# Three loads of the gate begun inside the next image's first norm, and two elementwise steps of the side work on GpSimd

## The chip, the cores and the metric

The kernel runs on one core of one Trainium2 chip. The metric is the time of one execution on the device in microseconds (us); where several executions are given, the median is used. A core has five engines that run side by side and wait for one another through semaphores: TensorE (PE; its weight loads are listed as PEld), VectorE (DVE), ScalarE (ACT), GpSimd (POOL) and SyncE (SP). In this kernel SP only issues DMA transfers. Each engine works through its own queue in order, so an instruction that waits holds up all that stand behind it on the same engine.

## What is computed

The input is 16 images of 256 channels by 32 x 32 positions, that is 256 x 1024 numbers an image, all in f32. Two layers follow one another, each behind a group norm:

```
x = x + attention_layer(group_norm(x))        # position, layer norm, 4 heads, feed-forward
x = x + scan_layer(group_norm(x))
# the scan layer, for one image:
xs    = xs + rel_h + rel_w
ctx   = sigmoid(conv3(xs) + gate_b)            # 256 channels
u, z  = split(xs @ in_proj.T)                  # 512 channels each
u     = silu(causal_conv4(u) + conv_b)
dt, Bm, Cm = split(u @ x_proj.T)
delta = softplus(dt @ dt_proj.T + dt_b)
h[t]  = exp(delta[t] * A) * h[t-1] + delta[t] * u[t] * Bm[t]    # 512 channels x 64 states
ys[t] = sum over states of h[t] * Cm[t]
y     = (ys + u * D) * silu(z)
out   = (y @ out_proj.T) * ctx
```

The two lines of code that change engine belong to `tok = group_norm(x) + position` at the head of the attention layer and to the product with `silu(z)` at the tail of the scan layer.

## The kernel before, in words

**The scan sets the beat.** The recurrence of one image has 512 x 64 rows of 1024 steps. They are cut into 256 units of 128 rows. The units of all images run one after another, 4096 in all, in the loop that begins at line 1000. Each unit takes one round of the loop, and a round writes, in this order:

- `load(n+6)` (line 900): SP fetches the unit's two rows of `delta*u`, spread over 128 partitions, into a buffer `dub`. There are seven such buffers; the one that is taken is free once `scan(n-1)` has read it.
- `inputs(n+4)` (line 905): POOL multiplies `dub` in place by `bt`, the rows of Bm.
- a step of `outputs` for the block of eight units that ended last (lines 947 to 963, on PE and ACT), which ends with two small stores to `ys` (line 970).
- `scan(n)` (line 922): DVE runs the recurrence over `a` (in PSUM) and `dub`.
- `decay(n+2)` (lines 914 and 916): PE spreads the pieces of delta into PSUM, and ACT takes the exponential. There are two buffers `a`, so the decay of unit n+2 can only begin when scan n is done.
- side work, below.

**The side work** is all that is not recurrence. While image b is scanned, the side work is, in this order: `first_norm(b+1)`, `gate_and_store(b-1)`, `attention_layer(b+1)`, `scan_inputs(b+1)`. Each is a generator that writes a few instructions and then yields a share; a share below 1 is that many rounds, and a larger one is at least one round and is divided by a rate (`gap`, `rate_for`, lines 980 to 988), which is chosen so that all shares of an image fill 247 rounds. The list GATE (line 811) gives the shares of `gate_and_store` for that sum. Image 0's side work runs alone ahead of the loop; while image 0 is scanned there is no gate; while image 15 is scanned there is only the gate of image 14; the gate of image 15 runs after the loop.

**The order on each engine.** PE, ACT, DVE and POOL keep the order in which the program writes their instructions (lines 1054 to 1058). On SP the compiler may put a transfer earlier, as long as its buffer and its data allow.

**The steps that the change touches.** `first_norm` sums both halves of the image (line 261), subtracts the mean (line 280), squares on ACT, sums again, takes the root on ACT (lines 291, 292) and multiplies (line 295); `along` writes one transfer after each step as long as there are some (two loads of the position). Then two DVE additions (line 362) make `tok`, and two stores keep it in DRAM (line 363). `gate_and_store` fetches `ys`, `w_o`, `ud` and `zs` of the first of four row groups, with a share of 0.4 after each (lines 822 to 824); then for each row group d it writes a load, the DVE instruction of line 830 (`us = us*D + ys`), a load, the DVE product of line 834 (`us = us*zs`), a load. The loads are three items further in the list each time. PE then multiplies by `w_o` (line 859) in eight steps, and DVE applies the gate and the residual (lines 846, 848). In the profile all tiles of the `wide` pool that a `fetch` fills are called `xs`; `xs<-ud` is the load of u for line 830, and `xs<-zs` that of z for line 834. The pool has ten buffers.

Of the kernel before, what the change touches and what calls it, by code (L numbers as in the profile page):

```python
# [14 lines left out]
ALU = mybir.AluOpType  # L15
# [14 lines left out]
ND = DI // P  # L30
# [20 lines left out]
def attention_then_scan_kernel(  # L51
# [18 lines left out]
    nc = tc.nc  # L70
    B = x.shape[0]
# [36 lines left out]
    def psum(name, dims=P):  # L108
        return (bank(mm, name) if beside["scan"] else free_bank(name))[:dims]
# [4 lines left out]
    def psum3(name):  # L114
        return bank(next(three), name) if beside["scan"] else free_bank(name)

    def work(name, n=L):
        return wide.tile([P, L + 2 + CONV], F32, name=name, tag="wide")[:, :n]
# [4 lines left out]
    def hs(h):  # L123
        return ts(h, HL)
# [6 lines left out]
    def col(name, i=0, n=1):  # L131
        o, w = _COLS[name]
        assert i + n <= w
        return vec[:, o + i : o + i + n]
# [104 lines left out]

    def along(steps, fetches):  # L240
        for share in steps:
            if fetches:
                fetches.pop(0)()
            yield share
        assert not fetches

    def grouped(ap):
        return ap.rearrange("p (h g t) -> p h g t", g=NG, t=2)

    def over_group(s):  # L250
        return s.unsqueeze(1).unsqueeze(3).to_broadcast([P, L // (2 * NG), NG, 2])
# [6 lines left out]
    def group_norm(src, dst):  # L258
        def sum_of(part, s, k):
            view = part.rearrange("p (h g t) -> p g h t", g=NG, t=2)  # L260
            nc.vector.tensor_reduce(s[:, k, :], view, AX.XY, ALU.add)

        def mean_of(s, name):
            m = psum(f"{name}_ps")[:, :NG]
            for k in range(KC):
                nc.tensor.matmul(m, avg, s[:, k, :], start=(k == 0), stop=(k == KC - 1))
            return m

        per = C / (C * L / NG)
        s = small.tile([P, KC, NG], F32, name="gn_s", tag="gn_s")  # L270
        sum_of(src[0], s, 0)
        yield 1
        sum_of(src[1], s, 1)
        m = mean_of(s, "gn_m")
        yield 1
        s = small.tile([P, KC, NG], F32, name="gn_q", tag="gn_s")
        qs = []
        nc.vector.tensor_scalar(m, m, per, None, ALU.mult)
        for k in range(KC):
            nc.vector.tensor_tensor(grouped(dst[k]), grouped(src[k]), over_group(m), ALU.subtract)  # L280
            q = work("gn_sq")
            nc.scalar.activation(q, dst[k], AF.Square)
            qs.append(q)
            yield 1
        sum_of(qs[0], s, 0)
        yield 1
        sum_of(qs[1], s, 1)
        del qs, q
        v = mean_of(s, "gn_v")
        yield 1  # L290
        nc.scalar.activation(v, v, AF.Ln, bias=eps, scale=per)
        nc.scalar.activation(v, v, AF.Exp, scale=-0.5)
        yield 2.2
        for k in range(KC):
            nc.vector.tensor_tensor(grouped(dst[k]), grouped(dst[k]), over_group(v), ALU.mult)
            yield 0.6
# [42 lines left out]
    state = [dict() for _ in range(B)]  # L339
# [6 lines left out]
    def fetches(to, src, n=KC):  # L346
        return [partial(fetch, to, src, k) for k in range(n)]


    def first_norm(b):  # L350
        xs, tok = [], []
        kept = state[b]["kept"] = dram.tile([C, L], F32, name="kept", tag="kept")
        if "x" in state[b]:
            xs = state[b].pop("x")
        else:
            for go in fetches(xs, x[b]):
                go()
            yield 0.4
        gn = [work("gn") for _ in range(KC)]
        yield from along(group_norm(xs, gn), fetches(tok, pos))  # L360
        for k in range(KC):
            nc.vector.tensor_tensor(tok[k], tok[k], gn[k], ALU.add)
            nc.sync.dma_start(kept[ts(k, P), :], tok[k])
            yield 0.6

# [442 lines left out]
        st["ys"] = dram.tile([DI, L], F32, name="ys", tag="ys")  # L808
        yield 1

    GATE = [0.4] * 4 + ([0.6, 0.6, 0.4] * ND)[:-1] + [1.3] * 8 + [1]

    def gate_and_store(b):
        st = state[b]
        (wo_s,), bring = weights((w_o, ND))
        ys, us, zs, gs, xs = [], [], [], [], []
        come = [
            partial(fetch, to, st[name], d)
            for d in range(ND) for to, name in ((ys, "ys"), (us, "ud"), (zs, "zs"))
        ]  # L820
        come.insert(1, bring[0])
        for go in come[:4]:
            go()
            yield 0.4
        come = come[4:] + [
            partial(fetch, to, st[name], k) for k in range(KC) for to, name in ((gs, "gs"), (xs, "xr"))
        ]
        for d in range(ND):
            come.pop(0)()
            nc.vector.scalar_tensor_tensor(us[d], us[d], col("D", d), ys[d], ALU.mult, ALU.add)  # L830
            ys[d] = None
            yield 0.6
            come.pop(0)()
            nc.vector.tensor_tensor(us[d], us[d], zs[d], ALU.mult)  # L834
            zs[d] = None
            yield 0.6
            if d + 1 < ND:
                come.pop(0)()
                yield 0.4
        if b + 2 < B:  # L840
            come += fetches(state[b + 2].setdefault("tok", []), state[b + 2]["kept"])
        ready = []

        def finish():
            for o, hf, ps in ready:
                nc.vector.scalar_tensor_tensor(ps, gs[o][:, hs(hf)], 1.0, ps, ALU.add, ALU.mult)
                t = xs[o][:, hs(hf)]
                nc.vector.scalar_tensor_tensor(t, ps, 0.25, t, ALU.mult, ALU.add)
                if hf == 1:
                    nc.sync.dma_start(out[b, ts(o, P), :], xs[o])  # L850
            ready.clear()

        for o in range(KC):
            for hf in range(2):
                ps = psum3("m_ps")
                for q in range(2):
                    first = o * HL + hf * 2 + q
                    for d in range(ND):
                        nc.tensor.matmul(  # L859
                            ps[:, ts(q, C)], us[d][:, ds(first, P, 4)], wo_s[:, d, :],  # L860
                            start=(d == 0), stop=(d == ND - 1),
                        )
                    if q == 1:
                        finish()
                    if come:
                        come.pop(0)()
                    yield 1.3
                ready.append((o, hf, ps))
        finish()
        del ps  # L870
        yield 1
        st.clear()


    units = [
# [27 lines left out]
    def inputs(n):  # L903
        v = loaded[n]
        nc.gpsimd.tensor_tensor(v, v, blocks[units[n][0]]["bt"], ALU.mult)  # L905
# [66 lines left out]
    def prepare(b):  # L972
        return chain(first_norm(b), attention_layer(b), scan_inputs(b))
# [6 lines left out]
    def gap(share, rate):  # L980
        return share if share < 1 else max(1.0, share / rate)
# [18 lines left out]
    for n, (b, k, q, e, i) in enumerate(units):  # L1000
        at = n % UNITS
        if at == 0:
            parts = [prepare(b + 1)] if b + 1 < B else []
            total = steps * len(parts)
            if b > 0:
                parts = [first_norm(b + 1), gate_and_store(b - 1), attention_layer(b + 1), scan_inputs(b + 1)]
                if b + 1 == B:
                    parts = parts[1:2]
                total = total + GATE
            side = chain(*parts)  # L1010
            rate, due = rate_for(total, UNITS - AHEAD - 3), 0.0
        if at == UNITS - AHEAD:
            for _ in side:
                pass
            if b + 2 < B:
                for go in fetches(state[b + 2].setdefault("x", []), x[b + 2]):
                    go()
        if n + AHEAD < len(units):
            load(n + AHEAD)
        if n + LEAD < len(units):  # L1020
            inputs(n + LEAD)
        if n % UNITS == SLOTS:
            spread_c(b, 1)
        if i == 0 and n > 0:
            running.insert(0, outputs(*units[n - 1][:4]))
        for g in list(running):
            if next(g, g) is g:
                running.remove(g)
        if n % UNITS == SLOTS - 1:
            spread_c(b, 0)  # L1030
        scan(n)
        if n + 2 < len(units):
            decay(n + 2)
        if at >= (1 if b + 1 < B else 8):
            due -= 1.0
            while due <= 0.0:
                due += gap(next(side, 1e9), rate)
# [76 lines left out]
```

## Time and profile before

| | |
|---|---|
| three runs | 13106.57 us median (13067.61, 13106.57, 13129.75) |
| the profiled execution | 13096.86 us, its span 13095.1 us |
| mean granted clock of TensorE | 0.80 of full speed |
| DVE busy | 11666.7 us |
| POOL busy | 9815.4 us |
| PE busy | 9717.3 us |
| ACT busy | 7520.3 us |
| transfers | 2820.10 MB, a mean of 215 GB/s |
| one image of the middle (5) | from 4421.6 to 5217.4 us, 795.8 us |

"Busy" counts the time in which an engine executes; waiting is left out. A group of the profile is a row such as `L834 DVE TENSOR_TENSOR xs<-xs 128x1024 ... x64 | 105.2, 1644 | 6.2`: line, engine, operation, what is written and read, how many, total busy us, mean ns of one, and the idle us of the engine just before them. The time of a DVE instruction in such a row includes any time in which it had started but could not reach its data. The list of waits names who waited for whom: total us, times, longest us. A row of the timeline gives start, length and instruction, with the idle time before it in brackets.

### The profile page before, as it was taken

What the parts mean: (1) busy time and instruction counts of PE and PEld (TensorE: products, weight loads), DVE (VectorE), ACT (ScalarE), POOL (GpSimd) and SP (SyncE); (2) the same over time, 40 slices, a digit from 0 to 9 for tenths busy, and PEclk for the clock granted to TensorE, in tenths of its full rate; (3) what the DMA queues carried; (4) which work ended last, traced back from release to release, by engine and by line L of the source; (5) the groups of instructions that cost most, each with busy time, mean ns of one, the idle gap of its engine ahead of it and who ended that gap; (6) DMA issues with size and microseconds to landing.
All of it is one profiled execution on the core that took longest, in us unless ns stands there. A gap on an engine that the chain in (4) does not pass through costs nothing.

```text
span 13095.1 us, 424083 instructions
## 1 busy us (share of the span) xinstructions
PE 9717.3 (74%) x186800; PEld 5456.0 (42%) x186800; DVE 11666.7 (89%) x7560; ACT 7520.3 (57%) x10421; POOL 9815.4 (75%) x4105
## 2 busy tenths in 40 slices
PE   6676876868778687786868767687686877868767
PEld 2344443444444344443444434444344444444445
DVE  3789999899999899988999898999989899889998
ACT  2465664655646556565665656566465664655654
POOL 0487876878778787786877768787687877878798
PEclk8887977879788697887879878797787977869755
DMA  1467666676666767666666666766667666676676
GB/s 52 165 220 238 208 218 218 220 243 201 221 216 219 235 200 233 216 220 231 211 224 218 213 223 213 236 210 219 218 218 234 205 218 217 218 236 204 227 248 231
DMA packets 1038401, 2820.10 MB, mean 215 GB/s; under 512 B 290370, under 2 KB 368451, under 8 KB 1036548
## 3 DMA queue, kind: packets, MB, share of 16 engines
q1 hardware_dynamic: 1036548, 2792.97, 64.6%
q8 instruction: 1459, 23.90, 0.7%
q14 instruction: 394, 3.23, 0.1%
HBM read 2513.82 MB, written 261.62 MB: 212 GB/s over the span
## 4 chain that ended last, share of the span: by engine, by line
DVE 36%; PE 31%; issue 13%; ACT 11%; DMA 6%; POOL 2%; SPq 1%; DVEq 0%; POOLq 0%; ACTq 0%
DVE h L922 25%; PE yb L947 6%; ACT a L916 5%; DVE mx L416 5%; PE a L914 5%; PE av L491 3%; PE g_ps L688 2%; DMA dub<-dus 2%; PE st_ps L503 2%; POOL dub L905 2%; PE z_ps L639 2%; PE yb L959 1%; PE m_ps L859 1%; PE qk_ps L403 1%; DVE u L674 1%
## 5 line engine op out<-in xcount | busy, mean ns | idle before, releaser
L905 POOL TENSOR_TENSOR dub<-dub,bt 128x1024 f32<-128x1024 f32 x4096 | 9810.6, 2417 | 3229.8 <-DMA dub<-dus 2896.6
L922 DVE TENSOR_TENSOR_SCAN h<-a,dub 128x1024 f32<-128x1024 f32 x4096 | 9215.1, 2278 | 752.0 <-ACT a L916 401.8
L916 ACT ACTIVATE a<-a,acol 128x1024 f32<-128x1024 f32 x4096 | 4462.8, 1090 | 3253.4 <-PE a L914 3206.7
L914 PE MATMUL a<-pieces,pick 48*128 48x512 bf16 x8192 | 1902.6, 455 | 2518.2 <-DVE h L922 2401.8
L947 PEld LDWEIGHTS yb<-h,cd 128*32 128x32 f32 x131072 | 2488.2, 128 | 2781.3 <-issue 1265.6
L947 PE MATMUL yb<-h,cd 128*32 128x64 f32 x131072 | 3255.8, 252 | 476.8 <-ACT y L953 325.2
L914 PEld LDWEIGHTS <-pick 48*128 48x128 bf16 x8192 | 603.3, 95 | 2915.4 <-issue 2467.5
L953 ACT COPY y<-yb 128x256 f32<-128x256 f32 x2048 | 763.6, 373 | 914.7 <-PE yb L947 907.5
L435 PE MATMUL s_ps<-k,q 32*64 32x512 f32 x4092 | 825.7, 619 | 95.5 <-DVE mx L416 95.0
L416 DVE TENSOR_REDUCE mx<-s_ps 128x1 f32<-128x512 f32 x1023 | 649.0, 681 | 15.5 <-PE s_ps L435 15.5
L491 PE MATMUL av<-pt,vv 128*64 128x512 f32 x2048 | 596.1, 662 | 3.0 <-ACT sums L480 1.7
L959 PE MATMUL yb<-turn,y 128*32 128x16 f32 x32768 | 591.4, 214 | 5.8 <-issue 4.9
L511 ACT ACTIVATE pt<-st_ps 128x512 f32<-128x512 f32 x1024 | 554.1, 599 | 60.9 <-PE st_ps L503 59.9
L959 PEld LDWEIGHTS yb<-turn,y 128*32 128x32 f32 x32768 | 573.8, 159 | 6.6 <-issue 5.2
L503 PE MATMUL st_ps<-sp 33*128 33x512 f32 x2048 | 561.8, 622 | 4.5 <-ACT pt L511 3.3
L963 ACT COPY yo<-yb 128x128 f32<-128x128 f32 x512 | 136.1, 266 | 587.8 <-PE yb L959 560.5
L688 PE MATMUL g_ps<-w,xp 128*128 128x256 f32 x1464 | 451.9, 447 | 0.0
L688 PEld LDWEIGHTS g_ps<-w,xp 128*128 128x128 f32 x1464 | 367.3, 326 | 65.5 <-issue 54.0
L435 PEld LDWEIGHTS s_ps<-k,q 32*64 32x64 f32 x4092 | 193.6, 131 | 440.8 <-DVE mx L416 421.1
L859 PE MATMUL m_ps<-w,xs 128*128 128x256 f32 x1024 | 317.5, 460 | 10.4 <-DVE xs L834 10.4
L674 DVE SCALAR_TENSOR_TENSOR u<-up,cwh,u 128x1024 f32<-128x1024 f32 x192 | 273.0, 1422 | 28.0 <-ACT u L666 27.7
L859 PEld LDWEIGHTS m_ps<-w,xs 128*128 128x128 f32 x1024 | 262.1, 328 | 55.9 <-issue 32.0
(177 smaller groups left out, 6690.8 us busy)
## 6 DMA issues: line engine op xcount, KB each, us to landing
dub<-dus SPq DMA_DIRECT2D x4096, 512.0 KB
dps<-pc SPq DMA_DIRECT2D x384, 128.0 KB
pieces<-dps SPq DMA_DIRECT2D x1024, 48.0 KB
xs<-in_x_dram SPq DMA_DIRECT2D x64, 512.0 KB
xs<-kept SPq DMA_DIRECT2D x64, 512.0 KB
zs<-z SPq DMA_DIRECT2D x64, 512.0 KB
ud<-u SPq DMA_DIRECT2D x64, 512.0 KB
dus<-du SPq DMA_DIRECT2D x64, 512.0 KB
```

The lines of the kernel that those rows point to most:

```text
L416: nc.vector.tensor_reduce(mx[:, g, c, hf : hf + 1], s, AX.X, ALU.max)
L435: nc.tensor.matmul(waiting[g][0][ts(e, 64)], q4[r, ts(c, 64)], k4[r, hs(hf)], start=True, stop=True,)
L491: nc.tensor.matmul(av[ts(e, 2 * DH)], vv[j // (NJ // 2)][:, j % (NJ // 2), 2 * pair + e, :], pts[e], start=(j == 0), stop=(j == NJ - 1),)
L503: nc.tensor.matmul(s, ka[r, ts(j, P)], qa[r, hs(hf)], start=True, stop=True)
L688: nc.tensor.matmul(ps[:, ts(q, C)], xp[k][:, ds(first + t, P, 4)], wg_s[:, k, t, :], start=(k == 0 and t == 0), stop=False,)
L905: nc.gpsimd.tensor_tensor(v, v, blocks[units[n][0]]["bt"], ALU.mult)
L914: nc.tensor.matmul(a[:, hs(hf)], w, pieces[r], start=True, stop=True)
L916: nc.scalar.activation(a, a, AF.Exp, scale=acol[:, at : at + 1])
L922: nc.vector.tensor_tensor_scan(now["h", e][:, i, :], decays.pop(n), loaded.pop(n), 0.0, ALU.mult, ALU.add)
L947: nc.tensor.matmul(yb[ts(g, 32), ts(s, 64)], cd[:, at // 16, ts(c, 32)], hbuf[:, :, at : at + 8], start=(c == 0), stop=(c == 1),)
L953: nc.scalar.copy(y2[:, r], yb[:, :256])
L959: nc.tensor.matmul(some[ts(r, 32), x], y2[:, r, x:256:8], turn[:, x], start=True, stop=True)
```

## The change

Three things are changed, for each image.

1. The first four items of the gate's loads (`ys`, `w_o`, `ud`, `zs` of row group 0) are handed to `first_norm` of the next image, which writes them after its sixth to ninth step: after the second sum of squares, after the root, and after each of the two multiplications of line 295. Their four shares of 0.4 are gone, so the gate's first DVE instruction comes directly behind the norm, and GATE is shorter by 1.6 rounds. Where there is no next image (the scan of image 15, and the gate of image 15 after the loop), the gate writes the four at its own start, without shares.
2. The product with z, four an image, is written for POOL.
3. The sum of norm and position, two an image, is written for POOL.

```
     def along(steps, fetches):
         for share in steps:
-            if fetches:
-                fetches.pop(0)()
+            go = fetches.pop(0) if fetches else None
+            if go:
+                go()
             yield share
...
-    def first_norm(b):
+    def first_norm(b, besides=()):
...
-        yield from along(group_norm(xs, gn), fetches(tok, pos))
+        yield from along(group_norm(xs, gn), fetches(tok, pos) + [None] * 3 + list(besides))
         for k in range(KC):
-            nc.vector.tensor_tensor(tok[k], tok[k], gn[k], ALU.add)
+            nc.gpsimd.tensor_tensor(tok[k], tok[k], gn[k], ALU.add)
             nc.sync.dma_start(kept[ts(k, P), :], tok[k])
...
-    GATE = [0.4] * 4 + ([0.6, 0.6, 0.4] * ND)[:-1] + [1.3] * 8 + [1]
+    GATE = ([0.6, 0.6, 0.4] * ND)[:-1] + [1.3] * 8 + [1]
 
-    def gate_and_store(b):
+    def gate_loads(b):
...
-        for go in come[:4]:
-            go()
-            yield 0.4
-        come = come[4:] + [
+        come += [
             partial(fetch, to, st[name], k) for k in range(KC) for to, name in ((gs, "gs"), (xs, "xr"))
         ]
+        st["gate"] = ys, us, zs, gs, xs, wo_s, come[4:]
+        return come[:4]
+
+    def gate_and_store(b):
+        if "gate" not in state[b]:
+            for go in gate_loads(b):
+                go()
+        ys, us, zs, gs, xs, wo_s, come = state[b].pop("gate")
         for d in range(ND):
             come.pop(0)()
             nc.vector.scalar_tensor_tensor(us[d], us[d], col("D", d), ys[d], ALU.mult, ALU.add)
             ys[d] = None
             yield 0.6
             come.pop(0)()
-            nc.vector.tensor_tensor(us[d], us[d], zs[d], ALU.mult)
+            nc.gpsimd.tensor_tensor(us[d], us[d], zs[d], ALU.mult)
...
-                parts = [first_norm(b + 1), gate_and_store(b - 1), attention_layer(b + 1), scan_inputs(b + 1)]
-                if b + 1 == B:
-                    parts = parts[1:2]
+                if b + 1 < B:
+                    parts = [
+                        first_norm(b + 1, gate_loads(b - 1)), gate_and_store(b - 1),
+                        attention_layer(b + 1), scan_inputs(b + 1),
+                    ]
+                else:
+                    parts = [gate_and_store(b - 1)]
```

More of the change, by code (lines that the diff above doesn't have):

```diff
@@ L871, in gate_and_store @@
         yield 1
-        st.clear()
+        state[b].clear()
     units = [
```

## The prediction

> **What bounds the kernel now.** I read the page first: engines, chain, groups.
>
> ```profile
> PE 9717.3 (74%) x186800; PEld 5456.0 (42%) x186800; DVE 11666.7 (89%) x7560; ACT 7520.3 (57%) x10421; POOL 9815.4 (75%) x4105
> ...
> DVE 36%; PE 31%; issue 13%; ACT 11%; DMA 6%; POOL 2%; SPq 1%; DVEq 0%; POOLq 0%; ACTq 0%
> ...
> L905 POOL TENSOR_TENSOR dub<-dub,bt 128x1024 f32<-128x1024 f32 x4096 | 9810.6, 2417 | 3229.8 <-DMA dub<-dus 2896.6
> L922 DVE TENSOR_TENSOR_SCAN h<-a,dub 128x1024 f32<-128x1024 f32 x4096 | 9215.1, 2278 | 752.0 <-ACT a L916 401.8
> ```
>
> DVE is the bound: 89% busy, with the scans 79% of its time. POOL is idle for 3230 us, nearly all of it waiting for the next `dub`, whose load waits for a scan. So an instruction taken off DVE should shorten the round, and POOL has room on the whole. Then the groups that change, and DVE's waits:
>
> ```profile
> L830 DVE SCALAR_TENSOR_TENSOR xs<-xs,vec 128x1024 f32<-128x1024 f32 x64 | 133.3, 2084 | 99.9 <-DMA xs<-ud 99.4 <-issue 0.3
> L834 DVE TENSOR_TENSOR xs<-xs 128x1024 f32<-128x1024 f32 x64 | 105.2, 1644 | 6.2 <-DMA xs<-zs 5.6
> L362 DVE TENSOR_TENSOR xs<-xs,gn 128x1024 f32<-128x1024 f32 x32 | 67.2, 2136 | 0.0
> ```
>
> The shortest of line 834 takes 1.19 us, so means of 1644 and 2136 ns hold something else. The timeline of image 5 shows what (POOL's row is from its own list):
>
> ```profile
> 4456.34 2.29 DVE L922 TENSOR_TENSOR_SCAN h<-a,dub 128x1024 f32<-128x1024 f32 x1 [1.42 <-POOL dub L905]
> 4458.55 4.48 DVE L362 TENSOR_TENSOR xs<-xs,gn 128x1024 f32<-128x1024 f32 x2
> 4462.95 4.46 DVE L922 TENSOR_TENSOR_SCAN h<-a,dub 128x1024 f32<-128x1024 f32 x2
> 4473.14 2.17 DVE L830 SCALAR_TENSOR_TENSOR xs<-xs,vec 128x1024 f32<-128x1024 f32 x1 [5.73 <-DMA xs<-ud]
> ...
> 4458.58 3.38 POOL L905 TENSOR_TENSOR dub<-dub,bt 128x1024 f32<-128x1024 f32 x1 [2.31 <-DMA dub<-dus]
> ```
>
> The two sums take 1.2 and 3.3 us: POOL's product and a DVE instruction with two inputs in SBUF don't run together. POOL's first lost 1 us to the first sum (3.38 for 2.36), and the second sum lasted until POOL was done. Scans, with one input in PSUM, keep their 2.28 us. At 4467.4 DVE stands 5.7 us until `ud` has landed. The worst of these is in image 15:
>
> ```profile
> 12461.00 11.29 DVE L830 SCALAR_TENSOR_TENSOR xs<-xs,vec 128x1024 f32<-128x1024 f32 x1 [3.62 <-DMA xs<-ud]
> ...
> 12455.01 16.20 POOL L905 TENSOR_TENSOR dub<-dub,bt 128x1024 f32<-128x1024 f32 x7
> ```
>
> POOL had seven products ready, ran them in one go to 12471.2, and DVE got its 1.25 us only then. Last, the stretches of image 5 (PE, PEld, DVE, ACT, POOL busy us and count, clock, DMA share, GB/s): up to scan 10, to the gate's last product, and the 12 units behind it.
>
> ```profile
> 4421.60:4456.30 34.70, 18.25 (x380) 12.26 (x379) 31.43 (x19) 18.69 (x25) 34.67 (x15) 0.50 0.74 244
> 4456.30:4501.30 45.00, 15.55 (x373) 10.46 (x372) 39.19 (x20) 12.04 (x16) 20.64 (x8) 0.54 0.79 283
> 4501.30:4541.80 40.50, 37.23 (x578) 26.62 (x578) 36.40 (x26) 16.40 (x22) 27.45 (x12) 0.91 0.80 265
> ```
>
> The 45 us are the place of the change: DVE 87% busy, POOL 46%, PE 35%.
>
> **The change part by part,** for each of images 1 to 14.
>
> *Taken off DVE.* Line 362: 2 x 2.14 = 4.3 us. Line 834: 4 x 1.64 = 6.6. The wait for `ud`: 99.4 / 16 = 6.2; it lies almost wholly at row group 0, whose three loads now stand behind the `dub` loads 11, 14 and 15 in SP's order instead of 17 and 18. That is 4438 to 4449 in image 5's time, 12 us and more before their use, in a stretch whose DMA share is 0.74. I cost them at nothing; the cover is POOL's lead over the scans there (inputs 12 ended 16 us before scan 12 began), and a `dub` delayed by one more transfer of 512 KB (1.9 us at 283 GB/s) would not reach it. Without that lead the three would cost 5.6 us. `w_o` stands at the same early place in SP's order as before. Sum: 17.1 us.
>
> *Added on POOL.* Six instructions of 2.36 us: 14.2. In the order of the changed kernel POOL has: inputs 14, both sums, inputs 15, product 0, inputs 16, 17, product 1, inputs 18, 19, product 2, inputs 20, product 3. From the sums to inputs 24 that is 16 x 2.36 = 37.8 us. Before, POOL finished inputs 14 at 4453.9 and scan 24 began at 4515.8: 62 us, and some 51 after the gain below. That leaves 13 us for standing still. Each product also waits for DVE's instruction ahead of it, and inputs behind it wait too; scans have four units of lead. I take no stall of scans from this. The stores of `tok` now wait for POOL: its sums should end by 4458.7, and the next `dub` load on SP is held for scan 10 until 4458.6 anyway, so nothing. PE waits for product 3, as it did on DVE; PE has done its decays by then and is 35% busy, nothing.
>
> *Waits that come in their place: loads.* The first four shares are gone, so DVE instruction 1 of line 830 now stands one scan behind instruction 0. From the end of scan 10 DVE has two scans (2 x 2.2) and one instruction (1.5) to do, 5.9 us. SP in the same time has to issue a `dub`, two small stores and `ys` ahead of this `ud`, about 2.3 us at 0.4 to 0.6 each. In the crowd the load took 7.3 us (issued 4465.87, used 4473.14), two `dub` beside it 6.6 and 9.4: mean 7.8. Wait: 2.3 + 7.8 - 5.9 = 4.2 us. From below, a `dub` in a quieter place took 4.7 us (4453.84 to 4458.58): 1.1. From above, 9.4: 5.8, and if all the transfers queue, more (rival 1).
>
> *Waits for POOL.* Line 830 has two SBUF inputs. Above 1.25 us it now loses 0.69 us a time (without the 11.29 us), 2.7 an image. After the change its four instructions can meet one, two, two and one inputs ahead of POOL's own next product, at most 6 x 2.36 = 14.2 us; at least nothing. I take half an instruction for the first and last, none for the second (it hides behind the load), one whole for the third: 4.7, so 2.0 more than now. Ends: -2.7 and +11.5. The Trainium skill (SBUF — State Buffer, Who interferes with whom) states that whichever of the two issues first holds the shared ports for the whole instruction and the other is blocked. The image-15 row agrees on blocking and goes further: DVE stayed out for more than four further products of POOL. By the page, with one instruction each, the upper end would be 4 x 2.36 - 2.7 = 6.7 us instead of 11.5; the forecast is the same.
>
> *Sum of an image:* 17.1 - 4.2 - 2.0 = 10.9 us. Not all passes through: image 0, with no gate, has 17.5 us less DVE work (709.5 against 727.0 us in image 5) and no 6.2 us wait, yet its 785.1 us (scan 0 at 435.5, the next image's at 1220.6) are only 15.9 below the mean of images 1 to 14, 801.0 (to 12434.3): 0.67. The rest came back as waits for decays. Here PE and ACT are mostly idle in the stretch, so I take 0.9: 9.8 us, times 14 = 137.
>
> *The rest.* Image 0 loses its two sums (1.22 and 3.30): -4. Image 15: four products of 5.5 us go; row group 0, which lost 3.6 and 10.0, waits up to 7.8 for loads that now go out unspaced, while POOL stops at its own product; group 1 waits up to 4: -7, between -19 and +5. The sums ahead of the loop and the last product behind it are on the path, 2.36 for 1.22: +3.
>
> Total: -137 - 4 - 7 + 3 = -145 us against the profiled execution's 13,096.9 (its span and 1.8 us), which is 10 us under the median of the three runs: **12,950 us**.
>
> **Rivals.** A change under 0.5% (65 us) can hardly be told from none here.
>
> 1. *Transfers bound the gate.* From the first store of `tok` to the last `ud` are 16 transfers of 512 KB. At the 283 GB/s of this stretch they need 29.6 us from 4456.4, plus 3 to land; instruction 3 ends at 4490.3. By my sum it ends at 4458.6 + 6 scans 13.2 + 5.0 + 4.7 + 4.2 = 4485.7. That gives 4.6 us back, 6.2 an image: 13,010. For it: the 0.79 share. Against: 20 us from 4480 on ran at 325 GB/s.
> 2. *The freed time becomes waits for decays* as in image 0, together with 1: 0.67 x 6.2 = 4.2 an image, 13,040 to 13,075: no change.
> 3. *The waits do not return:* loads land in time and DVE meets no more of POOL than now: 17.1 x 14 + 8 = 247: 12,850. Against: SP's issue order above.
> 4. *Slower: POOL becomes the bound between the first norm and unit 24.* If its six instructions cost the scans their full 14.2 us, and at each product POOL stands one scan long (4 x 2.2) because DVE got its turn late, 23 us replace 17.1: +6 an image, 13,180. It decides when POOL's new work and its standing take over 17.1 us from the scans. For it: the 11.29 us row and POOL's 34.67 busy us of 34.70 up to scan 10. Against: 46% busy in the gate, and inputs 16 ready 27 us before scan 16. The Trainium skill (GPSIMD Engine Reference, Engine selection) speaks for this one: it puts elementwise adds on VectorE, since GpSimd takes about twice as long; here 2.36 against 1.19 us.
>
> **How the numbers follow.** Forecast 0.58; rival 1 0.10 (faster); rival 2 0.13; rival 3 0.08; rival 4 0.11. Faster by over 0.5%: 0.58 + 0.10 + 0.08 = 0.76; within: 0.13; slower: 0.11. The range leaves out rival 4 and what lies beyond rivals 2 and 3: 12,850 to 13,080. The forecast alone, with its loads between 1.1 and 5.8 and half of POOL's bounds, spans 12,890 to 13,010.
>
> **What would show it.** Right: 64 products and 32 sums on POOL near 2.4 us; in image 5 from the start of scan 10 to that of scan 19 some 34 us where it was 45; a wait of line 830's successor for `ud` at the second row group, not the first; the stores of `tok` not holding SP; DVE's busy time 180 us less. Wrong: scans waiting for POOL around units 16 to 24 (rival 4); DVE's waits for ACT grown by as much as it lost (rival 2); waits for `ud` at three groups of four (rival 1).

## The result, and the profile after

The change made the kernel faster: 12999.29 us median of five runs (12970.68 to 13022.06) against 13095.71 (five runs of the kernel before, 13067.61 to 13129.75). The ratio is 0.9926, with a 95% interval of 0.9902 to 0.9949. The profiled execution has a span of 12997.4 us where it was 13095.1: 97.7 us less, not the 145 of the forecast. The mechanism is the one described; a third of the gain that was forecast got lost on the way, and the experiments look for where.

From the page of the changed kernel, the engines, the chain by engine, and the two costliest groups:

```profile
PE 9794.6 (75%) x186800; PEld 5486.9 (42%) x186800; DVE 11576.5 (89%) x7464; ACT 7531.4 (58%) x10421; POOL 10007.5 (77%) x4201
...
DVE 37%; PE 29%; issue 13%; ACT 10%; DMA 7%; POOL 3%; SPq 1%; DVEq 0%; POOLq 0%; ACTq 0%
...
L911 POOL TENSOR_TENSOR dub<-dub,bt 128x1024 f32<-128x1024 f32 x4096 | 9781.6, 2410 | 2841.4 <-DMA dub<-dus 2555.3
L928 DVE TENSOR_TENSOR_SCAN h<-a,dub 128x1024 f32<-128x1024 f32 x4096 | 9217.0, 2280 | 798.1 <-ACT a L922 492.2
```

DVE has 96 instructions fewer (64 products and 32 sums), and POOL 96 more. But DVE's busy time is only 90 us less: the two removed groups alone took 105.2 + 67.2 = 172.4 us. Something on DVE has become longer. The groups (line, engine, operation, count; busy us and mean ns; idle us before them and who ended it) show what. First those that the change touches:

```profile
L840 POOL TENSOR_TENSOR xs<-xs 128x1024 f32<-128x1024 f32 x64 | 150.6, 2354 | 94.3 <-DMA xs<-zs 54.5 <-DVE xs L836 22.3 <-issue 16.0
L836 DVE SCALAR_TENSOR_TENSOR xs<-xs,vec 128x1024 f32<-128x1024 f32 x64 | 116.7, 1824 | 124.5 <-DMA xs<-ud 124.1 <-issue 0.2
L363 POOL TENSOR_TENSOR xs<-xs,gn 128x1024 f32<-128x1024 f32 x32 | 74.8, 2360 | 32.2 <-DVE gn L296 32.2
```

The moved instructions take 2.35 and 2.36 us on POOL, as costed. DVE's instruction (line 830 before, 836 now) got shorter, from 133.3 to 116.7 us; its wait for `ud` grew from 99.4 to 124.1.

Then three groups of `scan_inputs`, a stage that the diff does not touch. Before:

```profile
L674 DVE SCALAR_TENSOR_TENSOR u<-up,cwh,u 128x1024 f32<-128x1024 f32 x192 | 273.0, 1422 | 28.0 <-ACT u L666 27.7
L717 DVE SCALAR_TENSOR_TENSOR u<-up,u 128x1024 f32<-128x1024 f32 x64 | 94.5, 1477 | 18.6 <-ACT up L712 18.6
L616 DVE TENSOR_TENSOR xp<-xp,xs 128x1024 f32<-128x1024 f32 x32 | 47.6, 1493 | 0.0
```

and after:

```profile
L675 DVE SCALAR_TENSOR_TENSOR u<-up,cwh,u 128x1024 f32<-128x1024 f32 x192 | 305.1, 1589 | 27.9 <-ACT u L667 27.7
L718 DVE SCALAR_TENSOR_TENSOR u<-up,u 128x1024 f32<-128x1024 f32 x64 | 116.7, 1823 | 18.6 <-ACT up L713 18.6
L617 DVE TENSOR_TENSOR xp<-xp,xs 128x1024 f32<-128x1024 f32 x32 | 88.6, 2809 | 0.0
```

The same instructions in the same number, all with two inputs in SBUF, take 32, 22 and 41 us longer: 95 us, nearly as much as the whole gain of the kernel.

To see where in an image the time went, I took the starts of the scans from the trace and cut each of images 1 to 14 into four stretches of units. Units 0 to 19 hold the end of the first norm and the gate up to its last product, 160 to 224 most of `scan_inputs`. Means in us:

| units | 0-19 | 19-160 | 160-224 | 224-256 | image |
|---|---|---|---|---|---|
| before | 79.4 | 419.1 | 200.4 | 102.1 | 801.0 |
| after | 68.4 | 416.2 | 207.7 | 101.9 | 794.3 |

The gate gained 11.0 us (the forecast said 10.9), and kept them: the attention stretch gained 2.9 more, and `scan_inputs` lost 7.3. That leaves 6.7 of 11.0. Each kernel's stretches come from its one profiled execution; a second profile of the changed kernel (below) has 68.3, 417.5, 205.7 and 102.2, so a difference of 1 to 2 us in a long stretch says little by itself.

### The profile page after: what moved, and what is told of

It is laid out like the page before. It is cut to its first block, busy times and chain, and to the rows that moved or that the text cites. A ratio compares the mean times of both kernels' runs of the same rounds, so it can differ in the third digit from the quotient of the medians.

```text
span 12997.4 us, 424123 instructions
## 1 busy us (share of the span) xinstructions
PE 9794.6 (75%) x186800; PEld 5486.9 (42%) x186800; DVE 11576.5 (89%) x7464; ACT 7531.4 (58%) x10421; POOL 10007.5 (77%) x4201
## 4 chain that ended last, share of the span: by engine, by line
DVE 37%; PE 29%; issue 13%; ACT 10%; DMA 7%; POOL 3%; SPq 1%; DVEq 0%; POOLq 0%; ACTq 0%
DVE h L928 26%; PE yb L953 5%; DVE mx L417 5%; ACT a L922 5%; PE a L920 4%; DMA dub<-dus 4%; PE av L492 3%; POOL dub L911 2%; PE st_ps L504 2%; PE z_ps L640 2%; PE g_ps L689 2%; PE yb L965 1%; PE m_ps L865 1%; DMA xs<-ud 1%; DVE u L675 1%
## 5 line engine op out<-in xcount | busy, mean ns | idle before, releaser
L689 PEld LDWEIGHTS g_ps<-w,xp 128*128 128x128 f32 x1464 | 369.1, 326 | 67.1 <-issue 58.1
L675 DVE SCALAR_TENSOR_TENSOR u<-up,cwh,u 128x1024 f32<-128x1024 f32 x192 | 305.1, 1589 | 27.9 <-ACT u L667 27.7
L865 PE MATMUL m_ps<-w,xs 128*128 128x256 f32 x1024 | 317.7, 460 | 11.8 <-POOL xs L840 11.8
```

The lines of the kernel that those rows point to most:

```text
L689: nc.tensor.matmul(ps[:, ts(q, C)], xp[k][:, ds(first + t, P, 4)], wg_s[:, k, t, :], start=(k == 0 and t == 0), stop=False,)
```

## The experiments

Two theories stood against each other for the missing time; the expectations below call them A and B.

- *Rounds* (A, spacing): the four shares that GATE lost move all the later side work. `scan_inputs` begins one round earlier (160 instead of 161 in image 6), and there its DVE instructions meet POOL's products in another way. In before, the two sums of line 616 are written in rounds 170 and 171 of an image; after the change, both in 170, back to back.
- *Pass-through* (B): DVE is not the only limit, so part of any gain in the gate comes back as waits for decays, wherever the later work stands. This was the prediction's reason for its factor 0.9.

**The rounds of before, with the change.** The four shares come back behind the gate's last product, where they delay nothing up to that product:

```
-    GATE = ([0.6, 0.6, 0.4] * ND)[:-1] + [1.3] * 8 + [1]
+    GATE = ([0.6, 0.6, 0.4] * ND)[:-1] + [0.4] * 4 + [1.3] * 8 + [1]
...
                 yield 0.4
+        for _ in range(4):
+            yield 0.4
```

> The change whole, but the four shares of 0.4 that it drops follow the gate's last product, so that all side work behind the gate stands in the same rounds as in the kernel before. Theory A (spacing): the gate stretch gave the 11 us an image that were summed, and 4 us of them went later because the side work behind it stands one to two rounds earlier against the scans, where DVE's two-input instructions of lines 617, 675 and 718 meet POOL's products more often (+42, +32 and +22 us in the changed kernel). Then this kernel has those three groups back near 47.6, 273 and 94.5 us and gains 10 to 11 us an image: 12,940 to 12,960 us. Theory B (limit elsewhere): DVE freed in the gate only reaches sooner what PE and ACT set, and the spacing does not matter: 12,985 to 13,015 us, with scans waiting some 490 us for ACT as in the changed kernel.

Measured: 12963.33 us, ratio 0.9908 (0.9886 to 0.9930), 3 us above the range of theory A and well below B's. That interval overlaps the one of the change, so the times alone do not part them; the stretches do: 68.1, 418.8, 201.1, 101.9, an image 789.9. From the groups of this kernel:

```profile
L675 DVE SCALAR_TENSOR_TENSOR u<-up,cwh,u 128x1024 f32<-128x1024 f32 x192 | 278.7, 1451 | 28.0 <-ACT u L667 27.7
L718 DVE SCALAR_TENSOR_TENSOR u<-up,u 128x1024 f32<-128x1024 f32 x64 | 91.5, 1430 | 18.6 <-ACT up L713 18.6
L617 DVE TENSOR_TENSOR xp<-xp,xs 128x1024 f32<-128x1024 f32 x32 | 46.2, 1448 | 0.0
```

All three groups are back near their old means, and `scan_inputs` at 201.1 us. DVE's busy time is 11479.0 us, 187.7 below before's, where the prediction's sign was 180. Of the 11.3 us that the gate gained, 11.1 now arrive at the end of the image (801.0 - 789.9). That speaks for the rounds.

**One part alone.** First the loads without the change of engine: both lines back to `nc.vector`.

```
-            nc.gpsimd.tensor_tensor(tok[k], tok[k], gn[k], ALU.add)
+            nc.vector.tensor_tensor(tok[k], tok[k], gn[k], ALU.add)
...
-            nc.gpsimd.tensor_tensor(us[d], us[d], zs[d], ALU.mult)
+            nc.vector.tensor_tensor(us[d], us[d], zs[d], ALU.mult)
```

> The early loads and the dropped shares alone; sum and product stay on DVE. If the wait for ud is really removed (6.2 us an image), 13,000 to 13,015 us. If it only moves to the second and fourth row group, as the changed kernel's trace has it, little is left: 13,070 to 13,095 us, and DVE's wait for ud stays at 60 to 120 us in all.

Then the kernel before with only these two lines changed, and so with the rounds and the loads of before:

```
-            nc.vector.tensor_tensor(tok[k], tok[k], gn[k], ALU.add)
+            nc.gpsimd.tensor_tensor(tok[k], tok[k], gn[k], ALU.add)
...
-            nc.vector.tensor_tensor(us[d], us[d], zs[d], ALU.mult)
+            nc.gpsimd.tensor_tensor(us[d], us[d], zs[d], ALU.mult)
```

> Sum and product on POOL alone; loads and shares as in the kernel before, so the rounds of the later side work are those of before. DVE loses 10.9 us an image of lines 362 and 834. Theory A: nearly all of it passes through, since the spacing is unchanged: 12,940 to 12,970 us. Theory B: about 0.6 of it: 13,000 to 13,015 us. In both the wait for ud at the first row group stays (5 to 7 us an image).

Measured: the loads alone 13062.54 us, ratio 0.9979 (0.9964 to 0.9994), between the two ranges that were set for it; the engines alone 13008.87, 0.9933 (0.9917 to 0.9950), inside the range of theory B, though not for B's reason, as the stretches show. In the gate they gain 79.4 - 73.0 = 6.4 and 79.4 - 72.1 = 7.3 us, together 13.7 where the change has 11.0: the two parts share 2.7 us. The waits of DVE for `ud` show why (total us, times, longest); the loads alone, then the engines alone:

```profile
DVE xs L836 <- DMA xs<-ud: 56.5, 25, 7.5
```

```profile
DVE xs L830 <- DMA xs<-ud: 178.2, 48, 9.1
```

Taking the product off DVE shortens the stretch in which the next `ud` lands, so the load is what is late next. Earlier loads nearly halve the old wait of 99.4 us; a faster DVE nearly doubles it. And the loads alone lose 6.4 us again in `scan_inputs` (206.8 us), having the shortened GATE, while the engines alone lose 0.6 (201.0). So an image of the first ends at 797.7, of the second at 794.4: moving the two operations gives on its own as much as the whole change (794.3). With the engines alone 6.6 of the 7.3 us of the gate reach the image's end: most of what is short of the 10.9 us of lines 362 and 834 was lost in the gate itself, where the wait for `ud` grew from 6.1 to 11.1 us an image.

The engines, one line of that diff at a time, first the sum (`tok`), then the product (`us`):

> The kernel before with the sum of norm and position on POOL, nothing else. In the mean of images 1 to 14 scan 11 begins 41.3 us after scan 0 in the kernel before: here 36.9 to 37.1, the 4.3 us of line 362. By scan 19 (79.4 before) 1 to 2 us of it is given back as a longer wait for ud at the first row group, whose loads still go out behind scan 10: 76 to 77 us. If the wait takes all of it, 79.

> The kernel before with the product with z on POOL, nothing else. By scan 19 it should be the 6.6 us of line 834 less what the loads of the second to fourth row group then are late: the kernel with both on POOL and the old loads had 4.0 us of waits for ud at row groups 3 and 4 and reached scan 19 at 72.1, 4.9 us of which I put down to the sum's 4.3. So 74 to 76 us. If the 6.6 us pass through whole, 72.8; if the loads take all, 79.

Measured: scan 19 starts 76.5 us after scan 0 with the sum alone, and 74.9 with the product alone, both within their forecasts; from the unrounded means the gains are 3.0 and 4.6 us, 7.6 together where both have 7.3. A single execution of each took 13075.1 and 13044.0 us beside a median of 13110.1 for the kernel before, and no interval belongs to these. In the gate each returns about two thirds of what it takes off DVE (4.4 and 6.8 us).

**Two more loads ahead.** To price the wait at the second row group: the rounds of before as above, and `ys` and `ud` of row group 1 handed to the norm as well (the four shares of the first experiment, and tests for an empty list, are in this kernel too and are left out here).

```
-        yield from along(group_norm(xs, gn), fetches(tok, pos) + [None] * 3 + list(besides))
+        yield from along(group_norm(xs, gn), fetches(tok, pos) + [None] + list(besides))
...
-    def gate_loads(b):
+    def gate_loads(b, ahead=6):
...
-        st["gate"] = ys, us, zs, gs, xs, wo_s, come[4:]
-        return come[:4]
+        st["gate"] = ys, us, zs, gs, xs, wo_s, come[ahead:]
+        return come[:ahead]
```

> As the kernel with the rounds of before, and two more loads (ys and ud of the second row group) handed to the first norm, each load of the gate thus two places earlier. If the waits for ud (124 us in the changed kernel) come from loads issued too late, they fall under 50 us, and the time is 50 to 80 us below that of the kernel with the rounds of before. If the transfers of the stretch bound it, the waits move on to the third and fourth row group and the time is within 25 us of it.

Measured: 12885.79 us, ratio 0.9840 (0.9821 to 0.9858); the gate 63.1 us, an image 786.7. Its wait for `ud`:

```profile
DVE xs L837 <- DMA xs<-ud: 54.1, 20, 9.3
```

Against 121.2 us with the same rounds and four loads ahead, 67.1 us went, 4.5 for each of the 15 gates in the loop, and the gate gained 68.1 - 63.1 = 5.0. The time is 77.5 us below that of the kernel with the rounds of before, as forecast for loads that are issued too late; the wait stayed just above the 50 us that went with it. The load waits of the changed kernel are a real price on the path.

**The loads alone, with the rounds of before.** The sharpest test of the rounds: the first experiment with both operations back on `nc.vector`. Beside it, the change was measured again on the same chip.

> The early loads alone, with sum and product on DVE, and the four dropped shares of 0.4 behind the gate's last product: the loads-only kernel with the rounds of before. Theory A (spacing): the 6.4 us an image that the loads-only kernel had gained at unit 19 are all left at the image's end, 12,995 to 13,015 us, and lines 617, 675 and 718 fall from 92, 303 and 109 us to about 47, 275 and 93. Theory B: no better than the loads-only kernel, 13,045 to 13,075 us.

> The changed kernel itself, beside the next three on the same chip, so that differences of a third of a per cent can be read: 12,980 to 13,020 us, and 5 to 8 us an image of the 11 us of the gate stretch left at the image's end.

Measured: 13045.68 us, ratio 0.9961 (0.9947 to 0.9975); the change again 12991.63, 0.9929 (0.9916 to 0.9942). The forecast of 12,995 to 13,015 was a miss, and the time lies at the lower end of what theory B allowed. The stretches say in which half: 72.9, 421.6, 201.1, 101.9. `scan_inputs` came back to 201.1 us as the rounds theory has it (from 206.8), and lines 617, 675 and 718 to 49.6, 272.2 and 96.2 us. But the attention stretch, 416.1 with the shortened GATE, became 421.6, slower even than before's 419.1.

So the rounds matter in that stretch too, in the other direction: it takes 416.1 to 417.5 us in every kernel whose attention layer follows the gate directly, and 417.7 to 421.6 in those with four shares or their old place ahead of it. One part of this shows in DVE's waits for the small transfers that carry the denominators of the attention layer to DRAM and back (`den`); before and after:

```profile
DVE few L535 <- DMA few<-den: 154.9, 15, 111.8
DVE ao L547 <- DMA sums<-den: 47.7, 11, 5.6
```

```profile
DVE few L536 <- DMA few<-den: 116.7, 12, 109.1
DVE ao L548 <- DMA sums<-den: 22.8, 16, 6.3
```

In units 19 to 160 these two cost some 1.0 to 1.7 us an image in the kernels with the early attention layer, and 5.1 to 5.8 in all others. The scans' waits for the decays go the other way there (20.2 before, 24.3 after), and those for `outputs` fall (7.6 to 4.8). The 2.5 us by which this kernel is slower than before are spread over several waits, two profiles of one kernel differ by half as much, and a part of the gate's gain coming back as waits, the other theory, is not excluded there.

That gives a kernel to try: the attention layer early, `scan_inputs` where it was.

**The four shares ahead of `scan_inputs`.**

```
-    GATE = ([0.6, 0.6, 0.4] * ND)[:-1] + [1.3] * 8 + [1]
+    GATE = ([0.6, 0.6, 0.4] * ND)[:-1] + [1.3] * 8 + [1] + [0.4] * 4
...
-                        attention_layer(b + 1), scan_inputs(b + 1),
+                        attention_layer(b + 1), [0.4] * 4, scan_inputs(b + 1),
```

> The change whole, with the four dropped shares put between the attention layer and the last stage of the side work (scan_inputs). So gate and attention stand in the rounds of the changed kernel, and scan_inputs in those of the kernel before. Theory A in its narrow form: what the changed kernel loses between units 160 and 224 (6.6 us an image against the kernel with all rounds kept) is the meeting of lines 617, 675 and 718 with POOL's products, and depends on the rounds of that stage alone; what it had gained up to unit 160 (13.9 us an image) then stays: 12,890 to 12,930 us, line 617 near 47 us. If only the whole schedule matters, or the loss is B's, 12,960 to 13,010 us.

The same with the two more loads:

> The kernel before this one with two more loads handed to the first norm (ys and ud of the second row group). If the 68 to 78 us that two more loads gave with all rounds kept add to it: 12,820 to 12,860 us. If the earlier start of the gate's product collides with the early attention steps, no better than 12,886 us, the two-more-loads kernel.

Measured: 12870.45 us, ratio 0.9842 (0.9827 to 0.9857), against 0.9929 for the change on the same chip; with the two more loads 12826.96, 0.9802 (0.9788 to 0.9816), the fastest kernel of the study. The stretches of the first are 68.0, 416.3, 201.8, 102.2: near the change's times in gate and attention, near before's in `scan_inputs`. (The rounds themselves are the change's only in part: the shares also alter the rate, so 11 DVE instructions of the attention layer of image 6 stand one or two rounds earlier than in the change. Those of `scan_inputs` are before's.) Its image is 788.2 us, 5.5 under the change's 793.7 on that chip; its profiled span (12908.2) lies at the upper end of its four runs (12866.24 to 12909.95), so the stretches may understate its gain. Those of the second are 63.1, 416.7, 198.6 and 102.0, an image 780.4. Against the change nothing was added but 1.6 rounds of rest. The first came out below its forecast of 12,890 to 12,930, the second within its 12,820 to 12,860.

**Only the two sums apart.** To pin the loss in `scan_inputs` to the meeting with POOL, the changed kernel with one edit: the second sum of line 617 goes one round later, all else stays.

```
             nc.vector.tensor_tensor(body[k], body[k], rels[k], ALU.add)
-            yield 0.6
+            yield 1.0 if k == 0 else 0.2
```

> The changed kernel with one instruction an image moved: the second sum of line 617 (norm and relative position) goes from round 170, where it stands behind the first, to round 171; the shares 0.6 and 0.6 behind the two become 1.0 and 0.2. If two DVE instructions with two SBUF inputs in the same round are what costs (the second lasts until POOL's product is done, as the two sums of line 362 did), line 617 falls from 90 to 45 to 55 us, and the time by 30 to 45 us, to 12,950 to 12,965. If the meeting is only a sign of a stretch that something else bounds, line 617 falls and the time stays within 15 us of the changed kernel's 12,992.

Measured: 12940.56 us, ratio 0.9872 (0.9856 to 0.9889), clear of the change's 0.9916 to 0.9942 and 9 us below the range that theory A gave. The timeline (start, length, instruction) of image 6 in the changed kernel, DVE and then POOL's row over it:

```profile
5720.77 2.28 DVE L928 TENSOR_TENSOR_SCAN h<-a,dub 128x1024 f32<-128x1024 f32 x1
5722.97 6.51 DVE L617 TENSOR_TENSOR xp<-xp,xs 128x1024 f32<-128x1024 f32 x2
5729.41 2.28 DVE L928 TENSOR_TENSOR_SCAN h<-a,dub 128x1024 f32<-128x1024 f32 x1
...
5715.81 15.87 POOL L911 TENSOR_TENSOR dub<-dub,bt 128x1024 f32<-128x1024 f32 x6 [0.93 <-DMA dub<-dus]
```

and with the sums apart:

```profile
5678.49 3.10 DVE L617 TENSOR_TENSOR xp<-xp,xs 128x1024 f32<-128x1024 f32 x1
5681.51 2.28 DVE L928 TENSOR_TENSOR_SCAN h<-a,dub 128x1024 f32<-128x1024 f32 x1
5683.71 1.19 DVE L617 TENSOR_TENSOR xp<-xp,xs 128x1024 f32<-128x1024 f32 x1
...
5673.53 13.58 POOL L911 TENSOR_TENSOR dub<-dub,bt 128x1024 f32<-128x1024 f32 x5
```

Two sums that take 1.19 us each when left alone need 6.51 back to back under a run of POOL's products, and 3.10 + 1.19 with a scan between them. The group fell to 58.8 us, short of the 45 to 55 of the forecast, from 88.6 in the first profile of the change and 93.6 in the second. The stretch 160-224 went to 203.8, between the changed kernel's (207.7 and 205.7 in its two profiles) and before's 200.4. The time fell by more than this one group: an image is 790.2 us, 3.6 less than in the second profile of the change, and line 617 gives 2.2 of it; no run explains the other 1.4.

Put together, the surplus of the three groups (lines 617, 675, 718, total over before's, divided by 16 images) follows the surplus of the stretch, us an image:

| kernel | 160-224 over before's 200.4 | three groups over before's |
|---|---|---|
| after | 7.3 | 6.0 |
| after, again | 5.3 | 4.9 |
| loads only | 6.4 | 5.5 |
| sums apart | 3.4 | 3.6 |
| shares ahead of scan_inputs | 1.4 | 1.6 |
| same rounds | 0.7 | 0.1 |
| engines only | 0.6 | 0.6 |
| sum alone (one execution) | 1.4 | 0.9 |
| product alone (one execution) | 1.9 | 1.0 |
| loads, same rounds | 0.7 | 0.2 |
| two more loads, same rounds | 0.8 | 0.3 |
| two more loads, shares ahead of scan_inputs | -1.8 | -0.2 |

So the theory of the rounds stands for `scan_inputs`. Pass-through as a fixed share falls: among the kernels with the rounds of before, 11.1 of 11.3 us arrived with the whole change, 6.6 of 7.3 with the engines alone, 14.3 of 16.3 with two more loads, and 3.5 of 6.5 with the loads alone. Most of what is missing in the last two is missing in the attention stretch, and stays open.

## Why the prediction was right or wrong

**What DVE was relieved of: right.** While images 1 to 14 were scanned (the gates of images 0 to 13) the sums had taken 4.4 us (4.3 forecast), the products 6.8 (6.6), the wait for `ud` 6.1 (6.2): 17.3 for 17.1.

**The new load waits: too small.** By row group the changed kernel waits 0, 3.91, 0.48 and 1.99 us in the same gates, 6.4 an image where I took 4.2. The second group was sized about right and in the right place, with SP's issue order as the reason. The fourth was missed: the sum looked at the first two row groups only, and the same catching-up happens again two groups later. The timeline of image 5 has it:

```profile
4447.40 1.26 DVE L836 SCALAR_TENSOR_TENSOR xs<-xs,vec 128x1024 f32<-128x1024 f32 x1
...
4454.23 2.59 DVE L836 SCALAR_TENSOR_TENSOR xs<-xs,vec 128x1024 f32<-128x1024 f32 x1 [3.37 <-DMA xs<-ud]
...
4461.71 1.97 DVE L836 SCALAR_TENSOR_TENSOR xs<-xs,vec 128x1024 f32<-128x1024 f32 x1 [0.52 <-DMA xs<-ud]
...
4470.51 1.83 DVE L836 SCALAR_TENSOR_TENSOR xs<-xs,vec 128x1024 f32<-128x1024 f32 x1 [2.46 <-DMA xs<-ud]
```

The first goes at once, the second and fourth stand for 3.37 and 2.46 us.

**Waiting for POOL in the gate: too large.** I added 2.0 us; the durations came to 1.42, 2.10, 1.93 and 1.99, above 1.25 us 2.4 together where before's had 3.0: 0.6 less. My split among the four failed, most of all "one whole for the third": it lost 0.7 us, not 2.36. The two errors (2.2 and 2.6) cancel nearly, so the 10.9 us of the sum met the 11.0 measured in part by luck.

**"Not all passes through ... I take 0.9": the step that failed.** 0.61 passed. The size was wrong, and more so the reason. From the list of waits after:

```profile
DVE h L928 <- ACT a L922: 492.2, 484, 8.6
DVE h L928 <- POOL dub L911: 127.7, 53, 8.2
...
DVE h L928 <- PE yb L953: 92.5, 87, 3.7
```

The scans' waits for decays (ACT's part) did grow, by 90.4 us (from 401.8), 6.1 an image. DVE's busy time fell by 90.2 us, so the sign that the prediction gave for rival 2 is there to the number. Yet the growth does not account for the lost gain: 4.0 of the 6.1 us lie in the attention stretch, which got 2.9 us shorter (PE's part, waits for `outputs` to have read `h`, fell by 63.8 us in all, from 156.3). And with the rounds kept the growth is 14.3 us, while the gate's gain is the same and 11.1 us arrive:

```profile
DVE h L930 <- ACT a L924: 416.1, 483, 9.1
```

The 4.3 us went with the re-timing of the stages behind the gate, +2.9 in the attention layer and -7.3 in `scan_inputs`, which the prediction did not look at, though it had said that GATE is shorter by 1.6 rounds and that this DVE operation and POOL's products shut each other out. For the same reason its sign "DVE's busy time 180 us less" failed in the change (90.2) and held with the rounds kept (187.7). Image 0's 0.67, which I had leant on, is near the 0.61, but no run gives the two a common cause: the change with the rounds kept had 0.98.

**The rest.** Image 0: -0.3 instead of -4; it had gained 4.0 by scan 19, had 2.4 left at unit 192 and nothing at unit 224, and no run explains that. I hadn't applied to it the loss that I had just read from it. Image 15: -5.5 instead of -7. The ends: -0.2 ahead of the loop and +2.3 behind the last scan, for +3. In sum 14 x 6.7 + 0.3 + 5.5 + 0.2 - 2.3 = 97.5, and by the unrounded means the 97.7 measured.

**What was costed at nothing.** It held nearly. The store of `tok` goes out at 4442.97 and 4445.27 us in image 5 and the next `dub` load 0.4 us after the second; PE waited for POOL's last products 11.8 us in the whole run, all of it behind the loop (10.4 for DVE's before). Scans waited 7.0 us in the whole run, five times, for what the list names as POOL's sums of line 363. POOL was busy 28.41 of 33.7 us in the gate:

```profile
4408.30:4443.00 34.70, 18.36 (x387) 12.33 (x380) 31.41 (x19) 18.99 (x26) 34.70 (x16) 0.50 0.85 291
4443.00:4476.70 33.70, 14.73 (x342) 9.97 (x341) 27.35 (x14) 11.65 (x15) 28.41 (x12) 0.55 0.93 338
4476.70:4517.10 40.40, 36.33 (x612) 26.29 (x611) 36.22 (x27) 18.49 (x25) 31.13 (x15) 0.99 0.78 257
```

(Columns as in the prediction.) Scan 10 to scan 19 took 33.7 us where 34 were announced, with DVE at 27.35 and the transfers at 0.93 of their time and 338 GB/s.

**The rivals.** Rival 1, transfers as the bound, is half there: waits at groups two and four, a DMA share of 0.93, and two more loads ahead gave 5.0 us. But the transfers ran at 338 GB/s, not at the 283 that its time assumed. Rival 2's time of no change did not come, though its sign did. Rival 3 fell with the waits of 6.4 us. Rival 4 did not happen: with the 7.0 us scans waited 134.6 us for POOL in place of 110.6, and in units 0 to 19, its place, 0.6 us an image in place of 1.3. The rule of the Trainium skill (GPSIMD Engine Reference, Engine selection) that elementwise adds belong on VectorE holds for the duration of one (2.36 against 1.19 us). For the kernel it led the wrong way: with DVE 87% busy and POOL 46% in that stretch, moving them gave a ratio of 0.9933. The price it speaks of was paid by an engine that had the time.

## What to carry to other kernels

Where side work is laid into a main loop by shares, taking shares away at one place re-times every stage behind it; compare the rounds of the later stages before and after, above all where two instructions fall together that stood apart, and put the freed shares just ahead of the stage whose timing was good. A stage that changes by a few us without being touched by the diff can be found by cutting the image at the starts of the main loop's instructions. When an operation leaves the bound engine, ask at each of its later repetitions, not only at the first, which load is late next.

## What was not expected of the hardware

Of two DVE instructions with two SBUF inputs, the second paid far more for POOL directly behind the first than with a scan between them. In images 1 to 14 the first sum of the pair in the changed kernel averages 2.52 us and the second 3.36; in the kernel with the sums apart the second averages 1.19, the time of one left alone. (The first stands behind a scan in both kernels, so a scan ahead is not enough to spare an instruction the wait.) 3.36 us is one product of POOL (2.36) and 1.0 more: the second sum seems to lose its turn to the product that the first had kept waiting. The Trainium skill (SBUF — State Buffer, Who interferes with whom) says that whoever issues first keeps the shared ports for the whole instruction; these rows agree with it for the second sum. Why a scan between them frees the second sum, and why the instruction of image 15 that the prediction shows stood behind more than four products, no run here settles.
